# Expert routing by token with rank matmuls, one expert applied to all rows, and logits moved into the second graph layer

## The chip, the cores and the metric

The kernel runs on one core of a Trainium2 chip. The core has a matrix engine (TensorE, "PE" in the profile, with its weight loads shown as "PEld"), a vector engine (VectorE, "DVE"), a scalar engine (ScalarE, "ACT"), GpSimd ("POOL") and a queue engine ("SP") that issues most of the transfers. Each engine works through its own instructions in order and waits on semaphores for the others. The time is device microseconds of that core; three runs of the kernel before took 965.22, 966.63 and 966.90 us, so the median is 966.63 us.

## The reference

A graph of 1250 nodes with 41,250 edges (20,000 random ones in both directions and a loop at every node) carries rows `x` of 512 floats. Two graph layers work on the normalised rows; each takes, at every node, the elementwise maximum over the rows of its neighbours, and two linear maps. Then comes a mixture of eight experts in which each expert chooses its 512 rows ("expert choice").

```python
def graph_conv_max(x, src, dst, W_rel, b, W_root):
    agg = segment_max(x[src], dst, num_segments=1250)
    return agg @ W_rel.T + b + x @ W_root.T
h = relu(graph_conv_max(layernorm(x), ...)); h = relu(graph_conv_max(h, ...))
x = x + h
y = layernorm(x)
probs = softmax(y @ Wr, axis=0)              # [1250, 8], over the rows
vals, idx = top_k(probs.T, 512)              # each expert's rows
hid = gelu(einsum('ecd,edf->ecf', y[idx], W1) + b1)      # 512 -> 256
out_e = einsum('ecf,efd->ecd', hid, W2) + b2             # 256 -> 512
x = x + zeros.at[idx].add(vals[..., None] * out_e)
```

Of equal probabilities the row that comes first is taken, as `top_k` does.

## The kernel before

Rows lie in ten tiles of 125 (`TN`, `NT`). `fast_gnn` does the graph layers, `expert_choice` the experts; a loop behind them runs a general version (`general_gnn`) only if the edges don't fit the fast one, which for these inputs they do.

**The graph layers.** In each layer `first_phase` does the bulk of the maximum with one-hot products on TensorE and gathers on POOL. `second_phase` finishes tile after tile: `own_rest` gathers and merges the last neighbours of a tile, `backs` merges what was put aside, `ended` then turns the tile (`turn`), multiplies it (`conv`) and starts a generator (`finish`) that is taken further, one `yield` at a time, whenever a later tile gets to `ended` (function `on`). In layer two `finish` is `residual` (lines 689 to 704): it loads the tile's rows of `x` and the root part of a tile to come; then adds the positive part of the product to `x` and takes the moments; then scales the row (`normed`) and stores it to `y_d` in HBM; then transposes it into `yT`. All instructions of `fast_gnn` go through the wrapper `InOrder`, which keeps them in the order of the program on their engine and gives them line 34 in the profile. `conv` takes its PSUM bank from `ps_m`, which has two.

Most tiles of layer two's work live in pools that are closed with `gctx`; `acc` (the rows) and `ohs` (one-hot masks; its front half is used again for `yT`) outlive them.

**The experts.** `expert_choice` (lines 1125 to 1370) isn't pinned: the framework's scheduler orders its instructions. It works in two layouts. In the first, partition 16e+r holds expert e, sixteen times the same, and the 1250 rows lie along the free dimension. There it computes, after layer two is done, the logits (12 products of 417 columns, line 1189), the softmax, and the bar, the smallest probability that an expert still takes (lines 1234 to 1254). The bar is searched on the bits of the float: eight rounds, in each of which the sixteen partitions of an expert try sixteen candidates for four bits. A round counts on DVE how many of 1250 values are at least the candidate (line 1242), and a product with `alike` (line 1247) sums over the sixteen.

Then, still along the free dimension, it marks the rows chosen and numbers them by running sums (`tensor_tensor_scan`, lines 1264 and 1267), adds the bias `b2` of all chosen experts to the rows by a product with the weighted mask (line 1275), and stores these rows to `out`. `by_token` transposes probabilities and places into the second layout, with a row per partition. `listed(e)` makes the list of expert e from it: ten one-hot comparisons of the place with a lane number (line 1303) and ten products (line 1304) with a payload of row number and probability, the latter as three bf16 parts.

`gathered` fetches the chosen rows of `y_d` by four indirect transfers of 128 rows (line 1319). `expert` loads the weights (lines 1326 and 1328), transposes the gathered rows (line 1333), multiplies by `W1` (line 1339), takes Gelu on ScalarE (line 1341), multiplies by `W2` (line 1346), scales by the probability on DVE (line 1349) and adds the result into `out` by four indirect transfers (line 1350). Adds of an expert wait until those of the expert before have landed. In the loop of lines 1365 to 1370 the list and the gather of expert e+1 are written ahead of the work of expert e.

Of the kernel before, what the change touches and what calls it, by code (L numbers as in the profile page):

```python
# [9 lines left out]
F32 = mybir.dt.float32  # L10
# [8 lines left out]
P = 128  # L19
# [22 lines left out]
def fast_gnn(tc, ctx, sh, io, y_d):  # L42
# [3 lines left out]

    nc = tc.nc
# [35 lines left out]
    yT = ohs.rearrange("p t n -> p (t n)")[:, :2 * KC * N].bitcast(F32).rearrange("p (c n) -> p c n", c=KC)  # L83
    flag_i = keep.tile([1, 1], I32, name="flag_i")
# [90 lines left out]

    xh = gw.tile([P, NT, 3, D], BF16, name="xh")
# [512 lines left out]
    def residual(t, pm):  # L689
        xt = gk.tile([P, D], F32, name="line", bufs=LINES)  # L690
        sp.dma_start(xt[:TN], x[t * TN:(t + 1) * TN, :])
        fetch_root(1, t + 3)
        yield
        dve.scalar_tensor_tensor(acc[:TN, t, :], pm[:TN], 0.0, xt[:TN], op0=ALU.max, op1=ALU.add)
        moments(t)
        spread(t, t + 1)
        yield
        inverted(t, t + 1)
        yn = gk.tile([P, D], F32, name="line", bufs=LINES)
        normed(t, yn[:TN])  # L700
        stored(y_d[t * TN:(t + 1) * TN, :], yn)
        yield
        turned(yn[:TN], yT[:, :, t * TN:(t + 1) * TN])
        yield

    def second_phase(layer, finish, beside):
# [52 lines left out]
        ready = (8, 9)  # L759
        ended(8, 9)  # L760
        while going:
            on()

# [16 lines left out]
    first_phase(1, 10, late_groups(1) + own_groups(1, range(EARLY)), set(range(NT)), blocks, ready_steps)  # L780
    second_phase(1, residual, lambda: None)
    gctx.close()
    return acc, yT, flag_i
# [341 lines left out]
def expert_choice(tc, ctx, sh, xs, yT, y_d, out):  # L1125


    nc = tc.nc
    ident, node_tile, rows = sh["ident"], sh["TN"], sh["rows"]
    wr, fw1, fb1_t, fw2, fb2 = sh["wr"], sh["fw1"], sh["fb1_t"], sh["fw2"], sh["fb2"]  # L1130
# [4 lines left out]
    TN = node_tile  # L1135
    NT = len(rows)
    CAP = min(512, N)
    R = P // E
    chunks = []
    step = (N + 2) // 3  # L1140
    for c0 in range(0, N, step):
        chunks.append((c0, min(step, N - c0)))
    rp = ctx.enter_context(tc.tile_pool(name="route", bufs=1))
    rp2 = ctx.enter_context(tc.tile_pool(name="route2", bufs=2))
    fwp = ctx.enter_context(tc.tile_pool(name="fwp", bufs=2))
    ps_t = ctx.enter_context(tc.tile_pool(name="fps_t", bufs=2, space=PSUM))
    ps_m = ctx.enter_context(tc.tile_pool(name="fps_m", bufs=3, space=PSUM))
# [3 lines left out]
    wr_s = rp.tile([P, KC, E], F32, name="wr_s")  # L1151
    nc.sync.dma_start(wr_s, wr.rearrange("(c p) e -> p c e", p=P))
    wr_rep = rp.tile([P, KC, E, R], F32, name="wr_rep")
    for c in range(KC):
        nc.gpsimd.tensor_copy(wr_rep[:, c], wr_s[:, c].unsqueeze(2).to_broadcast([P, E, R]))
    alike = rp.tile([P, P], F32, name="alike")
    nc.gpsimd.memset(alike, 1.0)
    alike_v = alike.rearrange("p (e r) -> p e r", r=R)
    nc.gpsimd.affine_select(out=alike_v, in_=alike_v, compare_op=ALU.is_ge, fill=0.0, base=0,
                            pattern=[[-R, E], [0, R]], channel_multiplier=1)  # L1160
    nc.gpsimd.affine_select(out=alike_v, in_=alike_v, compare_op=ALU.is_ge, fill=0.0, base=R - 1,
                            pattern=[[R, E], [0, R]], channel_multiplier=-1)
    lane_i = rp.tile([P, 1], I32, name="lane_ii")
    nc.gpsimd.iota(lane_i, pattern=[[0, 1]], base=0, channel_multiplier=1)
    cand = rp.tile([P, 8], I32, name="rcand")
    for i, shift in enumerate((26, 22, 18, 14, 10, 6, 2, 0)):
        nc.vector.tensor_single_scalar(cand[:, i:i + 1], lane_i, R - 1 if shift else 3,
                                       op=ALU.bitwise_and)
        if shift:
            nc.vector.tensor_single_scalar(cand[:, i:i + 1], cand[:, i:i + 1], shift,  # L1170
                                           op=ALU.logical_shift_left)
    lanes_b = rp.tile([P, P], BF16, name="lanes_b")
    nc.gpsimd.iota(lanes_b, pattern=[[1, P]], base=0, channel_multiplier=0,
                   allow_small_or_imprecise_dtypes=True)

    fb1_s = rp.tile([P, E * FC], F32, name="fb1_s")
    nc.scalar.dma_start(fb1_s, fb1_t)
    fb2_s = rp.tile([P, D], F32, name="fb2_s")
    nc.vector.memset(fb2_s, 0.0)
    for e in range(E):  # L1180
        nc.scalar.dma_start(fb2_s[e * R:e * R + 1, :], fb2[e:e + 1, :])

    prob = rp.tile([P, N], F32, name="prob")
    sm = rp.tile([P, 12], F32, name="sm")
    pls = []
    for k, (c0, w) in enumerate(chunks):
        pl = ps_m.tile([P, D], F32, name="pm")
        for c in range(KC):
            nc.tensor.matmul(pl[:, :w], wr_rep[:, c, :, :].rearrange("p e r -> p (e r)"),
                             yT[:, c, c0:c0 + w], start=(c == 0), stop=(c == KC - 1))  # L1190
        nc.vector.reduce_max(sm[:, k:k + 1], pl[:, :w], axis=AX.X)
        pls.append(pl)
    nc.vector.reduce_max(sm[:, 3:4], sm[:, 0:len(chunks)], axis=AX.X)
    nc.vector.tensor_scalar_mul(sm[:, 4:5], sm[:, 3:4], -1.0)
    nc.vector.memset(sm[:, 5:8], 0.0)
    for k, (c0, w) in enumerate(chunks):
        nc.scalar.activation(prob[:, c0:c0 + w], pls[k][:, :w], AF.Exp, bias=sm[:, 4:5],
                             accum_out=sm[:, 5 + k:6 + k])
    nc.vector.reduce_sum(sm[:, 8:9], sm[:, 5:8], axis=AX.X)
    nc.vector.reciprocal(sm[:, 9:10], sm[:, 8:9])  # L1200
    nc.vector.tensor_scalar_mul(prob, prob, sm[:, 9:10])


    pcol = rp.tile([P, NT, E], F32, name="pcol")
    nc.vector.memset(pcol, 0.0)

    def by_token(of, into, only=None):
        for t in range(NT):
            r = rows[t]
            pt = ps_t.tile([P, KC, P], F32, name="pt")  # L1210
            nc.tensor.transpose(pt[:r, 0, :], of[:, t * TN:t * TN + r], ident)
            nc.scalar.copy(into[:r, t, :],
                           pt[:r, 0, :].rearrange("p (e r) -> p e r", r=R)[:, :, 0])

    by_token(prob, pcol)
    pay = rp.tile([P, NT * E, 5], BF16, name="pay")
    pay4 = pay.rearrange("p (t e) k -> p t e k", e=E)
    lane_f = rp.tile([P, 1], F32, name="lane_f")
    nc.gpsimd.iota(lane_f, pattern=[[0, 1]], base=0, channel_multiplier=1,
                   allow_small_or_imprecise_dtypes=True)  # L1220
    nc.vector.tensor_copy(pay[:, :, 0], lane_f[:, 0:1].to_broadcast([P, NT * E]))
    tile_f = rp.tile([P, NT], F32, name="tile_f")
# [9 lines left out]


    base = rp.tile([P, 1], I32, name="base")
    nc.vector.memset(base, 0)
    jk = rp.tile([P, N], F32, name="jk")
    for i, shift in enumerate((26, 22, 18, 14, 10, 6, 2, 0)):
        last = shift == 0
# [237 lines left out]
```

## Time and profile before

| what | value |
|---|---|
| median of three runs | 966.63 us (965.22 to 966.90) |
| the profiled execution's own time | 959.5 us |
| its span, first to last instruction | 957.8 us |
| TensorE busy, share of the span | 680.2 us, 71% |
| DVE busy | 669.3 us, 70% |
| POOL busy | 531.3 us, 55% |
| ACT busy | 144.1 us, 15% |
| mean granted TensorE clock | 0.914 |

The profiled execution was some 7 us faster than the median of the timed runs; sums that are made on its trace are carried over to the median as differences.

How the profile's lines are read: a line of the timeline gives the start in us from the span's start, the length in us (of the whole group where several instructions are merged), the engine, the line of the kernel, the operation, the tile written and the tiles read, the shape, how many, and in square brackets how long the engine had been idle and what ended that. A line of the groups gives the same names, then busy time in all and mean nanoseconds of one, and the idle time before. In the row of slices each digit is the busy share of a fortieth of the span in tenths. "PEclk" is the clock that TensorE was granted, as a share of its full one. An f32 product appears as two records.

### The profile page before, as it was taken

How to read it: one execution, taken by the hardware profiler on the slowest of the kernel's cores; microseconds unless marked ns; L12 is line 12 of the kernel's file. 1: busy time of each engine (PE TensorE's matmuls, PEld its weight loads, DVE VectorE, ACT ScalarE, POOL GpSimd, SP SyncE). 2: the span in 40 equal slices, each digit the busy share in tenths (PEclk: the TensorE clock that was granted, in tenths of full speed). 3: DMA queues.
4: the chain of work that ended last, by engine and by line, in shares of the span. 5: the costliest groups of instructions: out<-in, count | busy, mean ns of one | idle time of the engine just before them, and what ended most of it. 6: DMA issues, size and time to landing. Idle time of an engine off the chain costs nothing. (4 is left out here: it accounts for less than half of the span.)

```text
span 957.8 us, 8211 instructions
## 1 busy us (share of the span) xinstructions
PE 680.2 (71%) x2367; PEld 359.4 (38%) x2367; DVE 669.3 (70%) x1248; ACT 144.1 (15%) x259; POOL 531.3 (55%) x528
## 2 busy tenths in 40 slices
PE   0000657798889978779888889877666156999992
PEld 0000323454455433335444545433233124454440
DVE  6799759999998866638999989976544773232211
ACT  0700000011000123111110000012222002122210
POOL 5653567776575677145777767777300004464642
PEclk9999978999999989879999999989877575999996
DMA  7428476967686778455978878778623015678773
GB/s 195 134 79 242 143 192 183 195 213 210 209 234 179 232 216 285 139 179 167 204 227 233 281 218 271 211 227 261 206 69 96 0 50 171 160 182 179 174 114 48
DMA packets 71001, 172.64 MB, mean 180 GB/s; under 512 B 12886, under 2 KB 17556, under 8 KB 70946
## 3 DMA queue, kind: packets, MB, share of 16 engines
q0 software_dynamic: 38368, 116.29, 45.5%
q1 hardware_dynamic: 31598, 54.60, 18.2%
q10 hardware_dynamic: 980, 1.12, 0.5%
q8 instruction: 21, 0.34, 0.1%
q14 instruction: 34, 0.28, 0.1%
HBM read 142.48 MB, written 29.45 MB: 180 GB/s over the span
## 5 line engine op out<-in xcount | busy, mean ns | idle before, releaser
L34 PE MATMUL pq<-xh,ohs 126*125 126x512 bf16 x1200 | 296.6, 391 | 66.1 <-DVE acc L34 64.3
L34 POOL DMA_INDIRECT hb<-table_d,late_i x214 | 227.1, 1061 | 128.2 <-issue 50.0
L34 DVE TENSOR_TENSOR acc<-acc,pq 125x1024 f32<-125x1024 f32 x180 | 219.3, 1218 | 45.1 <-PE pq L34 38.6
L34 PEld LDWEIGHTS <-ohs 126*125 126x125 bf16 x1200 | 165.9, 140 | 217.2 <-issue 145.0
L34 POOL DMA_INDIRECT hb<-table_d,nat_i x140 | 148.2, 1058 | 67.7 <-issue 33.2
L1319 POOL DMA_INDIRECT ysel<-y_d,idx x32 | 31.0, 970 | 114.2 <-PE pi L1304 72.8
L34 PE MATMUL pm<-wrel,turn 128*125 128x512 f32 x160 | 82.0, 660 | 14.1 <-DVE acc L34 11.7
L34 PE MATMUL pm<-wroot,turn 128*125 128x512 f32 x160 | 85.9, 619 | 0.0
L34 ACT COPY acc<-pq 125x1024 f32<-125x1024 f32 x20 | 20.2, 1012 | 357.1 <-PE pq L34 357.1
L34 DVE TENSOR_TENSOR wide<-wide,hb 125x1024 f32<-125x1024 f32 (+1 forms) x60 | 71.5, 1191 | 1.8
L1350 POOL DMA_INDIRECT out<-oo,idx x32 | 50.4, 1574 | 25.7 <-DVE oo L1349 13.1
L34 DVE TENSOR_TENSOR hb<-hb 125x1024 f32<-125x1024 f32 (+2 forms) x55 | 52.7, 958 | 16.7 <-DMA hb<-table_d,nat_i 16.7
L1349 DVE TENSOR_SCALAR oo<-pm,val 128x512 f32<-128x512 f32 x32 | 23.9, 750 | 57.4 <-PE pm L1346 57.4
L1339 PE MATMUL pm<-yselT,w 128*128 128x512 f32 x128 | 57.6, 603 | 1.1 <-ACT yselT L1334 1.0
L1346 PE MATMUL pm<-w,hT 128*128 128x512 f32 x128 | 57.7, 599 | 0.0
L34 DVE TENSOR_TENSOR wide<-hb 125x1024 f32<-125x1024 f32 (+1 forms) x40 | 48.1, 1201 | 6.4 <-DMA hb<-table_d,nat_i 6.3
L34 PEld LDWEIGHTS pm<-wrel,turn 128*125 128x125 f32 x160 | 32.0, 210 | 53.3 <-issue 46.5
L34 PE MATMUL pt<-ident,loc 125*20 125x125 f32 x10 | 3.2, 386 | 61.3 <-DVE loc L34 60.9
L1346 PEld LDWEIGHTS pm<-w,hT 128*128 128x128 f32 x128 | 23.7, 190 | 32.8 <-issue 26.5
L34 PEld LDWEIGHTS pm<-wroot,turn 128*125 128x125 f32 x160 | 31.6, 198 | 10.9 <-issue 2.3
L1339 PEld LDWEIGHTS pm<-yselT,w 128*128 128x128 f32 x128 | 24.0, 193 | 29.3 <-issue 27.1
L34 ACT COPY turn<-pt 128x500 f32<-128x500 f32 x40 | 22.9, 574 | 56.6 <-PE pt L34 56.5
(222 smaller groups left out, 696.6 us busy)
## 6 DMA issues: line engine op xcount, KB each, us to landing
w<-in_fw SPq DMA_DIRECT2D x16, 512.0 KB
ohs<-idx_d SPq DMA_DIRECT2D x10, 615.2 KB
ahead<-table_d SPq DMA_DIRECT2D x20, 250.0 KB
root_d<-line SPq DMA_DIRECT2D x20, 250.0 KB
ahead<-root_d SPq DMA_DIRECT2D x20, 250.0 KB
ovf_d<-line SPq DMA_DIRECT2D x18, 224.0 KB
hb<-table_d,late_i POOLq DMA_INDIRECT x214, 5.9
line<-in_x SPq DMA_DIRECT2D x10, 250.0 KB
```

What stands on the lines that cost most here:

```text
L34: made = call(*args, **kwargs)
L1319: nc.gpsimd.indirect_dma_start(out=ysel[:, c, :], out_offset=None, in_=y_d[:, :], in_offset=bass.IndirectOffsetOnAxis(ap=idx[:, c:c + 1], ...
L1339: nc.tensor.matmul(ph[:, :CAP], w1[:, k, f * P:(f + 1) * P], yselT[:, k, :], start=(k == 0), stop=(k == KC - 1))
L1346: nc.tensor.matmul(po, hT[:, f, c * P:(c + 1) * P], w2[:, f, :], start=(f == 0), stop=(f == FC - 1))
L1349: nc.vector.tensor_scalar_mul(oo, po, val[:, c:c + 1])
L1350: add = nc.gpsimd.indirect_dma_start(out=out[:, :], out_offset=bass.IndirectOffsetOnAxis(ap=idx[:, c:c + 1], axis=0), in_=oo[:, :], in_off ...
```

## The change

1. **Logits in layer two.** A new class `Routing` (`head`) holds the routing's constants and results, in the part of `ohs` behind `yT` and in `xh`, which moves to the pool that outlives layer two. `residual` gets a further step that computes the logits of its tile (`head.logits`: four products of 125 columns, a copy on ScalarE, a `reduce_max` on DVE). The rows of `x` are loaded by `fetch_x` three tiles ahead, into six tiles of the spare part of `ohs`. The constants are made in `head.constants`, called before the last two tiles are finished.
2. **One expert on all rows.** Expert 0 (`DENSE = 1`) isn't gathered. `dense_steps` is a generator of 22 steps: 12 with two f32 products each of `yT` by `W1` (500 or 375 columns), with a Gelu after every second, and 10 with a bias product and two f32 products by `W2`, and a copy. Four steps stand at the end of layer two, two behind the exponential, one in each round of the bar search but the first, three among the ranks, and the last six behind the list of expert 1. `own_row` adds the result, times `gate` (the probability if the row is chosen, else zero), to the rows and stores them to `out`, beside expert 1.
3. **The bar.** A round has one DVE instruction less on its way (the shift is taken into the product), and the bar is summed up in two halves, which a product spreads into the second layout. The transposes of the probabilities stand in round one.
4. **Places by token.** The rows chosen are marked and numbered in the second layout: `ranks` sums a mask over the rows ahead of each by products with a triangle and with ones. The scans, the wide masks and the second `by_token` go.
5. **Lists.** `listed` makes the ten one-hot masks of an expert in one DVE instruction of 1280 elements, and its payload in another of 200.
6. **Biases.** `b2` is kept as three bf16 parts in one tile of 96 partitions, and `bias` adds it by one bf16 product into each output of an expert; the ten f32 products of line 1275 go.
7. **Order and buffers.** `expert_choice` is pinned to program order as `fast_gnn` is. Weights have three buffers, and are loaded two experts ahead; the PSUM pool `ps_m` has four banks. `expert` is a generator of two parts (up to Gelu, and the rest).

```diff
@@ fast_gnn
     def residual(t, pm):
-        xt = gk.tile([P, D], F32, name="line", bufs=LINES)
-        sp.dma_start(xt[:TN], x[t * TN:(t + 1) * TN, :])
+        xt = x_tiles[t % 6]
         fetch_root(1, t + 3)
+        fetch_x(t + 3)
         yield
...
         turned(yn[:TN], yT[:, :, t * TN:(t + 1) * TN])
+        yield
+        head.logits(t, ps_q.tile([P, R, D], F32, name="pq")[:, 0, :])
         yield
...
+        if layer == 1:
+            head.constants()
         ended(8, 9)
         while going:
             on()
+            if layer == 1 and len(going) < 2:
+                head.beside(2)
@@ Routing
+    def logits(self, t, pl):
...
+        for c in range(KC):
+            pe.matmul(pl[:, :r], self.wr_rep[:, c].rearrange("p e r -> p (e r)"),
+                      self.yT[:, c, t * TN:t * TN + r], start=(c == 0), stop=(c == KC - 1))
+        act.copy(self.prob[:, t * TN:t * TN + r], pl[:, :r])
+        dve.reduce_max(self.tops[:, t:t + 1], self.prob[:, t * TN:t * TN + r], axis=AX.X)
+    def dense_steps(self):
...
+                    for k in range(KC):
+                        pe.matmul(ph[:, :w], w1[:, k, f * P:(f + 1) * P], self.yT[:, k, c0:c0 + w],
+                                  start=(k == 0), stop=(k == KC - 1))
+                        if k % 2:
+                            yield
+                    act.activation(self.hT[:, f, c0:c0 + w], ph[:, :w], AF.Gelu,
+                                   bias=self.fb1_s[:, e * FC + f:e * FC + f + 1])
@@ expert_choice
+    act.activation(prob, prob, AF.Exp, bias=sm[:, 1:2], accum_out=sm[:, 2:3])
...
+    beside(2)
+    dve.reciprocal(sm[:, 3:4], sm[:, 2:3])
+    dve.tensor_scalar_mul(prob, prob, sm[:, 3:4])
+    act.copy(bp[:B3], fb[:B3])
+    pool.tensor_sub(fb[:B3], fb[:B3], bp[:B3])
+    act.copy(bp[32:64], fb[32:64])
+    act.copy(mid[64:B3], fb[64:B3])
+    pool.tensor_sub(fb[64:B3], fb[64:B3], mid[64:B3])
+    act.copy(bp[64:B3], fb[64:B3])
...
+        pe.matmul(pn, alike, sat, start=True, stop=True)
+        if i == 0:
+            for t in range(NT):
...
+                pe.transpose(pt[:r, 0, :], prob[:, t * TN:t * TN + r], ident)
+                act.copy(pcol[:r, t, :], pt[:r, 0, :].rearrange("p (e r) -> p e r", r=R)[:, :, 0])
+        else:
+            beside()
...
+    def ranks(of):
+        pr = ps_m.tile([P, D], F32, name="pm")
+        flat = of.rearrange("p t e -> p (t e)")
+        pe.matmul(pr[:, :NE], head.low, flat, start=True, stop=False)
+        for t in range(1, NT):
+            pe.matmul(pr[:, t * E:NE].rearrange("p (t e) -> p t e", e=E), head.ones,
+                      of[:, t - 1, :].unsqueeze(1).to_broadcast([P, NT - t, E]),
+                      start=False, stop=(t == NT - 1))
...
     def listed(e):
+        pays = rp2.tile([P, NT, CC, 5], BF16, name="pays")
+        dve.tensor_tensor(pays, pay4[:, :, e, :].unsqueeze(2).to_broadcast([P, NT, CC, 5]),
+                          col4[:, :, e, :].unsqueeze(3).to_broadcast([P, NT, CC, 5]), op=ALU.mult)
+        oh = rp2.tile([P, NT, P], BF16, name="oh")
+        dve.tensor_tensor(oh, head.lanes_b.unsqueeze(1).to_broadcast([P, NT, P]),
+                          lane[:, :, e].unsqueeze(2).to_broadcast([P, NT, P]), op=ALU.is_equal)
...
         for c in range(CC):
             po = ps_m.tile([P, D], F32, name="pm")
+            bias(po, e, P)
...
+    for _ in head.steps:
+        pass
+    for e in range(DENSE, E):
+        work = expert(e, *made, ysel)
         if e + 1 < E:
+            nxt = listed(e + 1)
+            ysel_n = gathered(nxt[0])
+        next(work)
+        if e == DENSE:
+            for t in range(NT):
+                own_row(t)
+        next(work)
```

## The prediction

> **What bounds the kernel now.** I read the page's slices first, for the stages, then the timeline of each engine from 620 us on, because the order of instructions up to there is unchanged by the diff. From the page: the slices of TensorE and its granted clock, and one group.
>
> ```profile
> PE   0000657798889978779888889877666156999992
> PEclk9999978999999989879999999989877575999996
> ...
> L34 POOL TENSOR_TENSOR xh<-acc,xh 125x512 bf16<-125x512 f32 x10 | 11.1, 1149 | 0.0
> ```
>
> One slice is 23.9 us. From slice 30 to 33 (718 to 814 us) TensorE is nearly idle and its clock is down to 0.5 to 0.7: the routing. Then come eight experts with TensorE at nine tenths or more. The timeline of the end of layer two:
>
> ```profile
> 683.70 0.69 DVE L34 SCALAR_TENSOR_TENSOR acc<-pm,line 125x512 f32<-125x512 f32 x1 [3.78 <-DMA line<-in_x]
> 690.51 0.69 DVE L34 SCALAR_TENSOR_TENSOR acc<-pm,line 125x512 f32<-125x512 f32 x1 [4.36 <-DMA line<-in_x]
> ...
> 697.65 1.90 PE L34 MATMUL pt<-ident,acc 125*128 125x125 f32 x8 [5.37 <-DVE acc L34]
> 699.38 5.88 PE L34 MATMUL pm<-wrel,turn 128*125 128x512 f32 x8
> 706.38 3.60 PE L34 MATMUL pm<-wrel,turn 128*125 128x512 f32 x8
> ```
>
> The residual adds of tiles 5 and 6 wait for loads of `x` (8.1 us together); the merges of tile 9 stand behind them on DVE, and `turn(8)`, `turn(9)` behind those. The product of tile 9 (706.38, plus its root part) ends at 710.85; I call this point T0. The routing, by its first and last lines:
>
> ```profile
> 720.60 10.48 PE L1189 MATMUL pm<-ohs,wr_rep 128*128 128x417 f32 x24 [2.35 <-POOL wr_rep L1155]
> 735.32 1.52 DVE L1242 TENSOR_SCALAR_CACHE_REDUCE jk<-prob,bound 128x1250 f32<-128x1250 f32 x1
> 757.72 1.52 DVE L1242 TENSOR_SCALAR_CACHE_REDUCE jk<-prob,bound 128x1250 f32<-128x1250 f32 x1
> 794.10 1.02 POOL L1319 DMA_INDIRECT ysel<-y_d,idx  x1 [72.85 <-PE pi L1304]
> 803.24 1.09 PE L1333 MATMUL pt<-ident,ysel 128*128 128x128 f32 x4 [6.83 <-DMA ysel<-y_d,idx]
> 906.08 1.04 PE L1333 MATMUL pt<-ident,ysel 128*128 128x128 f32 x8
> 908.69 7.13 PE L1339 MATMUL pm<-yselT,w 128*128 128x512 f32 x16 [0.19 <-ACT yselT L1334]
> 915.66 7.22 PE L1346 MATMUL pm<-w,hT 128*128 128x512 f32 x16
> 922.71 1.04 PE L1333 MATMUL pt<-ident,ysel 128*128 128x128 f32 x8
> ```
>
> So: T0 to the bar search 24.5 us; the search 25.1 (to 760.46); from there to the first expert's transposes 42.8; experts 803.24 to 939.51 = 136.3, each 16.63 (906.08 to 922.71) as TensorE alone sets it; then 18.3 to the end of the span.
>
> **Layer two.** Two edits act against each other. `x` is loaded three tiles ahead, which takes both waits away. But each tile now has its logits (8 records of 128x125) on TensorE behind the product four tiles later, a copy on ScalarE, and a `reduce_max` on DVE ahead of the next residual add; and the next-but-one product waits for that add, since `ps_m` has two buffers. So a loop closes: product 4.4 us (639.22 to 643.6), logits, copy 0.27, maximum 0.29, `inverted` 0.35, add 0.7, latencies 0.2. Logits of 125 columns have no row: the f32 records of 417 columns above run at 0.35 us warm, which scales to 0.105; the weight load in front of each is 0.19. Bounds 0.8 and 2.4 us a tile; I take 1.6, eight weight loads, since that is the longer of two overlapping things. Loop 7.8 us.
>
> Placed on the timeline: the add of tile 3 goes from 667.08 to 668.05, of tile 4 from 673.27 to 675.9, of tile 5 stays at 683.7, of tile 6 goes from 690.51 to 691.5. What prefetching gives, the maxima take: merges of tile 9 at 693.4 (692.36 before), `turn(8)` at 698.6. The product of tile 8, as cold as now, ends at 706.9 (706.1); then logits(4), copy, maximum, and only then the add of tile 7 at 709.65, which the product of tile 9 waits for. T0 becomes 714.85: **+4.0**. The DVE constants (nine of 0.15) and the Pool constants lie in the waits of 5 and 35 us there. On SP's queue the `x` loads now stand ahead of the stores of `y`, and the first expert's weights (1 MB) and `fb1` ahead of its last four; they land long before the dense steps at 728. A transfer met uncovered there would cost what the wait for `x` did: 6.2 (issued 684.25, used 690.5).
>
> **T0 to the bar search.** The tail was a ping-pong of `turned` and `normed` of about 2.3 us; with logits it is 2.8, four times (turned 0.6, copy 0.58, logits 1.6), and the last logits end at T0+12.9. Ahead of the exponential, ScalarE's queue now holds a Gelu of the dense expert: it waits for four f32 products of 500 columns (8 x 0.42 = 3.4), T0+16.3; Gelu 0.7; table load 1.28; exponential over 1250 columns 1.4 (417 take 0.61, of which 0.26 is fixed): ends at E = T0+19.8. Reciprocal and scaling 1.2: search at T0+21.0 = 735.9 against 735.32, so **-3.5** for this stage. It saves 10.5 of matmuls and gives most back.
>
> Here a rule weighs. The row: a table load takes 1.28 us, and the work ahead of it at 809.13 ended 0.01 before. The Trainium skill (ScalarE: Activation LUTs, section What ACT_TABLE_LOAD costs) gives 1283 ns plus about 1380 ns of drain for every switch of set. Before, both switches lay in waits; after there are three, two of them (exponential, second Gelu) on the path. By the row 1.28 each as taken; by the page +2.8 in all. I take the row and keep 2.8 in the range.
>
> **The bar search.** An iteration is now 3.16 us (735.32 to 738.48); the shift (0.19) goes, `add` and `ahead` fit in the 0.68 wait for TensorE: 2.97. But in iteration 1 the product `pn` stands behind ten transposes, whose ScalarE copies stand behind: table load 1.28, Gelu 0.7, four bias copies of 0.6 and two Pool subtractions of 1.15 (the group above): 7.0 after E. Ten copies at 0.83 a pair end at E+11.2, where `pn` was wanted at E+5.9. Search ends at E+12.4 + 5 x 2.97 + 1.56 + 1.5 = E+30.3, which is 29.1 long against 25.1: **+3.9**. Call the end B = 764.9. The dense steps between (4 records of 0.31 = 1.25 us) fit even at half clock.
>
> **B to the first expert.** Removed: 14 us of 1250-wide DVE work, ten f32 bias products and their adds. Added: some 19 DVE instructions on 8 to 320 elements (0.2 to 0.5 us by neighbours like the 0.24 of 128x80), two rank groups of eleven small bf16 products (0.1 each), and dense steps between them: 1.95 us each (four f32 records of 0.43 and a bf16 one of 0.22). Chain: masks B+2.9, ranks behind two dense steps B+5.3 and B+8.2, then DVE 3.9 of which the one-hot over 1280 elements is 1.49 (0.16 + 1280/0.96 GHz, the slope of the 1250-wide rows; 0.83 if packed in pairs), list, gather at B+13.7 (now 33.6). The rows would be there at B+22, but six dense steps (11.7) and the next list come first on TensorE: transposes at B+25.9 = 790.8. Against 42.8: **-16.9**. Own rows (7 us of DVE) and their ten stores lie beside the first expert's 17 us; the scatters have about 11 us of slack before a buffer is missed.
>
> **Experts.** Seven instead of eight: 136.3 less 16.6 and less 3.2 (the first, cold one) = 116.4. The bias adds four bf16 products of 0.213 each: 7 x 0.85 = 6.0. Lists were interleaved with transposes and free. Now order is pinned: the list for e+1 stands ahead of the transposes of e on TensorE, and on DVE behind the four `oo` of e-1. TensorE waits for the last `oo` 0.78, `pays` 0.33, one-hot 1.45, 0.1 latency, then ten products 0.7: 3.3 at five boundaries = 16.6. Sum 139.0: **+2.7**. Queued behind the list are transposes and so the whole expert; Pool (12.6 busy) has room.
>
> **Sum.** +4.0 - 3.5 + 3.9 - 16.9 + 2.7 = -9.8 on the span of 957.8. That execution itself took 959.5, below the 965.2 to 966.9 of the runs; I carry the difference over: 966.6 - 9.8 = **956.9**.
>
> **Rivals.** (1) *The logits are cheap*: at 0.9 us a tile, ten times on the chain, -7: 950. For it: weight loads are hidden in wide products; against: at 125 columns they are the longer part. (2) *TensorE's clock*, the slower one. For it: the clock was 0.50 in 735 to 760, and the product at 699.38 ran at half speed after a wait of 5.37. The skill (TensorE: Matmul & The Clock Gate, Part 1) says a window of 3.4 us of idling halves it and one of work restores it. The boundary stall of 2.6 and sparse 3.3 behind it may fill a window: 1.7 x 5 = 8.5; the steps after the bar at half clock: 7.5 (three rank steps +1.9, one warm-up +1.7). All: 973; from 12 of the 16 on, the result is slower. Against: the dense steps fill TensorE to about half in the search, more after. By the row of the experts (1.00 granted, gaps under 1 us) nothing is lost, which I take. (3) *Stores hold the scatters*: if `out` is written over 11 us later than reckoned, each further microsecond counts; 957 to 966. For it the ten stores took 13.3 before; against, the slack.
>
> **Numbers.** Likeliest 0.45 (951 to 963), (1) 0.15, (2) 0.32, (3) 0.08. Measurement tells 0.2% (1.9 us) from no change. Faster: 0.42 + 0.15 + 0.03 + 0.03 = 0.63; slower 0.22 of (2) and 0.04 of the rest = 0.26; same 0.11. Range 945 to 974: it leaves out the low half of (1) and the worst of (2).
>
> **What would show it.** DVE's residual adds free of `in_x` but waiting for ScalarE; T0 near 715; the exponential behind a Gelu; a gap of about 5 us in iteration 1 of the search; first gather some 14 us after the bar; TensorE waiting about 2.6 us for the one-hot at five expert boundaries, period 20.8. Wrong if logits take under 1 us, if the clock falls at the boundaries, or if dense steps delay each `pn`.

## The result

The changed kernel takes 959.99 us (median of 20 runs, 951.97 to 967.42) against 965.15 us (20 runs, 960.15 to 969.75) for the kernel before: a ratio of 0.9937, 95% interval 0.9916 to 0.9958. A second measurement of the same kernel, told below, gave 0.9976 (0.9952 to 1.0), so the gain is real but small. All ratios here leave out executions more than 1.5% above the fastest of their kernel, and where two kernels are compared below in us, the difference is taken between their ratios. The prediction was 956.9 us. The profiled execution took 962.38 us, its span is 960.6 us.

The two profiles differ by 7.2 us before the change begins to act: the first residual add of layer two starts at 641.88 us before and at 649.07 us after, though the diff alters nothing ahead of it but where `xh` lies and a few loads. So stages are compared by their lengths, not by clock times:

| stage | before | after | difference | predicted |
|---|---|---|---|---|
| first residual add to T0 (end of tile 9's product) | 68.96 | 69.04 | +0.1 | +4.0 |
| T0 to the first pass of the bar search | 24.5 | 21.4 | -3.1 | -3.5 |
| bar search | 25.1 | 26.5 | +1.3 | +3.9 |
| bar to the first expert's transposes | 42.8 | 22.7 | -20.1 | -16.9 |
| experts, to the end of TensorE | 136.3 | 154.4 | +18.1 | +2.7 |
| sum | | | -3.7 | -9.8 |

The slices of the page after, 24.0 us each (TensorE, and its granted clock):

```profile
PE   0000657898899978779888889868867888788892
PEclk9999877799999979879999999989978798988897
```

The gap of the routing (slices 30 to 33) is filled: TensorE is at seven and eight tenths there. But the experts behind it, slices 34 to 38, are at 7, 8, 8, 8, 9 where they were at nine tenths throughout, and their clock is at 9, 8, 8, 8, 9. The timeline after, layer two and the routing:

```profile
681.29 0.28 DVE L34 TENSOR_REDUCE ohs<-ohs 128x1 f32<-128x125 f32 x1 [6.40 <-ACT ohs L34]
688.75 0.69 DVE L34 SCALAR_TENSOR_TENSOR acc<-pm,ohs 125x512 f32<-125x512 f32 x1
696.11 0.69 DVE L34 SCALAR_TENSOR_TENSOR acc<-pm,ohs 125x512 f32<-125x512 f32 x1
710.89 1.05 PE L34 MATMUL pq<-ohs 128*128 128x125 f32 x8
...
734.86 0.68 ACT L34 ACTIVATE xh<-pq,ohs 128x500 f32<-128x500 f32 x1 [2.36 <-PE pq L34]
735.56 1.28 ACT L34 ACT_TABLE_LOAD   x1
736.85 1.34 ACT L34 ACTIVATE ohs<-ohs,sm 128x1250 f32<-128x1250 f32 x1
739.49 1.52 DVE L34 TENSOR_SCALAR_CACHE_REDUCE jk<-ohs 128x1250 f32<-128x1250 f32 x1
748.93 0.16 DVE L34 TENSOR_SCALAR step_i<-pn 128x1 int32<-128x1 f32 x1 [2.46 <-PE pn L34]
778.07 2.25 POOL L34 DMA_INDIRECT ysel<-y_d,idx  x1 [26.69 <-issue]
788.68 1.07 PE L34 MATMUL pt<-ident,ysel 128*128 128x128 f32 x8
```

No residual add waits for `x` any more; the maximum ahead of it waits for ScalarE's copy of the logits. The exponential stands directly behind a Gelu and a table load. The first gather goes out 12.1 us after the bar (765.97) instead of 33.6. And the experts:

```profile
800.92 0.75 DVE L34 TENSOR_SCALAR oo<-pm,val 128x512 f32<-128x512 f32 x1 [4.73 <-PE pm L34]
...
819.97 1.65 POOL L34 DMA_INDIRECT out<-oo,idx  x1 [25.61 <-DMA w<-in_fw]
825.02 0.75 DVE L34 TENSOR_SCALAR oo<-pm,val 128x512 f32<-128x512 f32 x1 [14.70 <-DMA out<-oo,idx]
880.16 0.41 PE L34 MATMUL pi<-pays,oh 128*128 128x20 bf16 x10 [2.52 <-DVE oh L34]
884.18 9.47 PE L34 MATMUL pm<-yselT,w 128*128 128x512 f32 x16 [0.68 <-ACT yselT L34]
903.92 0.41 PE L34 MATMUL pi<-pays,oh 128*128 128x20 bf16 x10 [2.52 <-DVE oh L34]
928.17 7.13 PE L34 MATMUL pm<-yselT,w 128*128 128x512 f32 x16 [0.68 <-ACT yselT L34]
```

From list to list (880.16 to 903.92) an expert takes 23.76 us, where 20.8 was reckoned and 16.63 was the period before. TensorE waits 2.52 us for the one-hot, as foreseen; what was not taken into the sum is the next line: the hidden product behind such a wait takes 9.47 us, and 7.13 where no wait stands ahead of it (928.17). The row of SP's queue that the scatters will be seen to depend on:

```profile
790.26 15.92 SPq L34 DMA_DIRECT2D out<-acc  x10
```

The ten stores of the own rows take 15.92 us to issue, so the last leaves near 806 us, and the loads of the weights for the next experts follow it on the same queue.

### The profile page after: what moved, and what is told of

The parts are those of the page before. It is cut to its first block, busy times and chain, and to the rows that moved or that the text cites. A ratio compares the mean times of both kernels' runs of the same rounds, so it can differ in the third digit from the quotient of the medians.

```text
span 960.6 us, 8344 instructions
## 1 busy us (share of the span) xinstructions
PE 709.5 (74%) x2484; PEld 375.0 (39%) x2484; DVE 648.1 (67%) x1164; ACT 154.5 (16%) x274; POOL 535.2 (56%) x543
## 5 line engine op out<-in xcount | busy, mean ns | idle before, releaser
L34 PEld LDWEIGHTS <-ohs 126*125 126x125 bf16 (+1 forms) x1221 | 168.1, 140 | 218.5 <-issue 147.2
L34 DVE TENSOR_SCALAR oo<-pm,val 128x512 f32<-128x512 f32 x28 | 21.0, 750 | 112.4 <-PE pm L34 92.9
L34 POOL DMA_INDIRECT out<-oo,idx x28 | 48.2, 1722 | 77.6 <-DVE oo L34 49.3
L34 PE MATMUL pm<-w,hT 128*128 128x512 f32 x112 | 52.6, 591 | 0.0
L34 POOL DMA_INDIRECT ysel<-y_d,idx x28 | 28.5, 1018 | 40.0 <-issue 33.4
L34 PE MATMUL pt<-ident,acc 125*128 125x125 f32 x80 | 14.0, 318 | 22.3 <-DVE acc L34 21.9
```

What stands on the lines that cost most here:

```text
L34: made = call(*args, **kwargs)
```

## The experiments

Three theories were to be told apart for the 15 us that the experts took beyond the sum: the clock after each boundary's wait, the stores of the own rows that hold the scatters (819.97, 18 us after `oo` was ready), or a limit of Pool and the transfers. Beside it: do the maxima take what the prefetch of `x` gives, and what is the dense expert worth?

The first four kernels ran on one chip. There the kernel before took 964.37 us (25 runs).

**The changed kernel again.**

> The changed kernel again, as the measure for the runs beside it: 960 us, 0.994 of the kernel before; nothing in it is altered.

961.99 us, 0.9976 (0.9952 to 1.0). Its stages: 72.35, 21.4, and experts 157.0. So the same kernel's stages differ by some 3 us between executions; the three that follow are read against this one.

**One maximum.** In `logits` and in `expert_choice`:

```
-        dve.reduce_max(self.tops[:, t:t + 1], self.prob[:, t * TN:t * TN + r], axis=AX.X)
...
-    dve.reduce_max(sm[:, 0:1], head.tops, axis=AX.X)
+    dve.reduce_max(sm[:, 0:1], prob, axis=AX.X)
```

> The ten maxima of 128x125 are taken out of layer two; one maximum over 1250 columns stands ahead of the exponential instead (about 1.5 us in place of 0.2). Theory A, as the prediction had it (the maxima take what the prefetch of x gives): the stage from the first residual add to the end of tile 9's product falls from 69.0 to about 63, and the kernel by 4 to 6 us against the changed one. Theory B, from the trace after (TensorE itself needs 4.5 for the product, 0.9 for the logits and 1.2 for transposes a tile, against a loop of 7.0): only about 0.5 us a tile is to be had, -2.5 in the stage, and with the longer maximum the kernel moves by -1.5 to +1 us.

946.9 us, 0.982 (0.9789 to 0.985): 15 us below the repeat, more than either theory gave. The stage up to T0 is 60.46 us (72.35), the way to the search 17.9 (21.4). Theory B counted only TensorE's own work of 6.6 us a tile against a loop of 7.0, and missed what stands behind an add. The maximum ahead of the add of tile t+1 belongs to logits that stand on TensorE behind the product of tile t+2: in the changed kernel the add of tile 4 starts at 681.75, though its product ended near 669.6. Without the maximum an add is free when its own product is done, and the merges of the last tiles, queued behind the adds on DVE, come early too: the transposes of tiles 8 and 9 start 49.0 us after the first add (693.20) instead of 54.2 in the profile after (703.24) and 57.4 in the repeat. TensorE's waits in 640 to 705 us of this kernel, in all (us, times, longest):

```profile
PE pm L34 <- DMA ahead<-root_d: 3.9, 3, 3.2
PE pm L34 <- DVE acc L34: 3.6, 2, 2.6
PE pt L34 <- DVE acc L34: 2.1, 1, 2.1
```

The waits for DVE are down to 5.7 us (the one at 703.24 alone was 7.50 in the changed kernel), and the next limit shows: the root rows arrive late. In the tail behind T0 the last logits start 8.8 us after it instead of 10.7, because no maximum stands in the ping-pong; the other 1.5 are products that ran warm (7.87 us for the 24 records from the last logits on, 9.34 in the profile after), which the next kernel has too, without this edit.

**`x` late.**

```
         xt = x_tiles[t % 6]
+        fetch_x(t)
         fetch_root(1, t + 3)
-        fetch_x(t + 3)
...
-    for t in range(3):
-        fetch_x(t)
```

> The rows of x are loaded when the residual of their own tile begins, as in the kernel before; all else is as changed. Theory A (the prefetch gives something that the maxima take): DVE waits for x again at tiles 5 and 6 on top of the maxima, the stage from the first residual add to the end of tile 9's product grows by 3 to 6 us, and the kernel by as much. Theory B (the waits were hidden anyway, since the maxima wait for later events): within 1 us of the changed kernel.

963.83 us, 0.9994 (0.998 to 1.0008): 1.7 us above the repeat, with intervals that overlap. The waits come back, but short:

```profile
675.89 0.69 DVE L34 SCALAR_TENSOR_TENSOR acc<-pm,ohs 125x512 f32<-125x512 f32 x1 [1.16 <-DMA ohs<-in_x]
685.57 0.69 DVE L34 SCALAR_TENSOR_TENSOR acc<-pm,ohs 125x512 f32<-125x512 f32 x1 [0.91 <-DMA ohs<-in_x]
```

Three of them, 3.1 us together with one of 1.00 at 654.74, in place of 8.1 before, and the stage is 3.0 us longer (75.39); the tail behind it was 2.8 us shorter in this execution. So in the changed kernel the prefetch is worth about these 3 us at most, which is no more than two executions of one kernel differ by in this stage (69.04 and 72.35). Taken together with the kernel before this one: with `x` early and the maxima away, the stage is 8.5 us shorter than before the change, about the two waits of 8.1; with the maxima in place it is not shorter at all. So the maxima do take what the prefetch gives. The fourth combination, `x` late without the maxima, was not run.

**Own rows early.** `own_row(t)` is moved from behind the first expert's hidden product into the loop that runs the remaining dense steps, after the second list's one-hot:

```
+    def own_rows():
+        done = 0
+        for _ in head.steps:
+            for t in range(done, head.ready):
+                own_row(t)
+            done = head.ready
...
-        if e == DENSE:
-
-            for t in range(NT):
-                own_row(t)
```

> The own rows (ten operations on DVE of 0.68 and their ten stores) follow the dense steps one by one, behind the one-hot of the second list, rather than standing behind the list: the first store leaves about 12 us earlier. Theory A (the stores hold the scatters and that costs): the first scatter starts near 803 us instead of 820, DVE's waits for the scatters of 19.6 us in all are gone, and the kernel gains 3 to 6 us. Theory B (the late scatters lie beside a boundary that TensorE loses to its clock anyway): the scatters move but the boundary between experts 2 and 3 becomes like the others, 23.8 us, and the kernel stays within 1.5 us.

954.69 us, 0.9887 (0.985 to 0.9925): 8.6 us below the repeat by the ratios, theory A and more. The experts take 144.0 us (157.0):

```profile
811.16 1.65 POOL L34 DMA_INDIRECT out<-oo,idx  x1 [15.23 <-DVE val L34]
831.68 0.41 PE L34 MATMUL pi<-pays,oh 128*128 128x20 bf16 x10 [2.52 <-DVE oh L34]
835.13 7.13 PE L34 MATMUL pm<-yselT,w 128*128 128x512 f32 x16 [0.68 <-ACT yselT L34]
852.53 0.41 PE L34 MATMUL pi<-pays,oh 128*128 128x20 bf16 x10 [2.52 <-DVE oh L34]
```

The first scatter starts 8.3 us earlier than in the repeat (819.45), not the 16 expected, but DVE no longer waits for scatters. Measured from first output product to first output product, the second boundary falls from 27.84 to 20.85 us: -7.0. Two more boundaries fall from 23.8 to 20.8, with the same wait of 2.52 us at each: at 831.68 the hidden product behind it runs at 7.13. So the wait of 2.52 us costs the clock at some boundaries and at others not, and 20.8, the period predicted, is what one costs where it doesn't. Of the 13.0 us between these two profiles, then, 7.0 are the boundary with the held scatters (the longer stop and the clock lost behind it) and 5.8 are two boundaries that happened to keep the clock.

That issuing the stores earlier helps is shown. At 819.97 the trace names the load of the next weights (`w<-in_fw`) as what ended the wait, but in the program that load stands behind the scatter. The last store landed at 816.41 by the semaphores of the trace, 3.6 us ahead of the scatter, and here at 807.75, 3.4 us ahead of the one at 811.16. So the stores are the likelier cause; what fills the last 3.5 us stays open.

The next four ran on another chip, on which the kernel before took 1033.71 us (13 runs); most of the difference lies ahead of the first residual add (at 695 to 704 us there), so ratios and stage lengths are read.

**List inside the hidden product.** `expert` yields once more, behind the first half of its hidden product, and the loop becomes:

```
         work = expert(e, *made, ysel)
+        next(work)
         if e + 1 < E:
             nxt = listed(e + 1)
             ysel_n = gathered(nxt[0])
         next(work)
```

> The list and the gathers for expert e+1 stand inside expert e, behind the first half of its hidden product, instead of ahead of its transposes. Theory A (the boundary costs its wait of 2.5 us and a cold clock behind it): no wait for the one-hot, the hidden product at 7.1 us in place of 9.0 to 9.6, the period 23.8 falls to about 17.9 (16.6 as before, 0.9 for the biases, 0.3 for the list), five boundaries give about 29 us: 930 us. Theory B (the period is set by Pool and the transfers, whose work is the same): Pool needs 12.8 us an expert, but the gathers land late, the transposes wait for them, the period is 20 to 22 and the time 940 to 950.

1012.78 us, 0.9779 (0.9673 to 0.9885). The period is 18.2 us at the undisturbed boundaries, theory A; no hidden product there is cold, and Pool carries the same work in 18.2 us, so theory B falls. But one boundary takes 35.2 us:

```profile
884.49 1.65 POOL L34 DMA_INDIRECT out<-oo,idx  x1 [25.41 <-DMA w<-in_fw]
892.07 1.02 POOL L34 DMA_INDIRECT ysel<-y_d,idx  x1 [0.30 <-issue]
896.37 1.94 PE L34 MATMUL pt<-ident,ysel 128*128 128x128 f32 x8 [13.09 <-DMA ysel<-y_d,idx]
```

The first scatters stand at the head of Pool's queue until the own rows are written; the gathers for expert 3 stand behind them, and TensorE waits 13.09 us for those rows.

**Boundary kept busy.** In `listed`, ahead of the list's products:

```
+        if e > DENSE + 1:
+            spare = head.bank()
+            for k in range(10):
+                pe.matmul(spare, pick[:B3, 0, :], bp[:B3, :], start=True, stop=True)
         for t in range(NT):
```

> Ten bf16 products of 96x512 into a spare bank stand ahead of the list at five boundaries, so that TensorE works while it waits for the one-hot; nothing reads them, and the wait itself stays. Theory A (idling costs the clock): the boundary stays at 2.5 us or a little longer, but the transposes take 1.1 and the hidden product 7.1 us, the period is 20.8 to 21.3 as the prediction had it, and five periods give 12 to 15 us: 946 us. Theory B (the hidden product is long for another reason, its operands or the transfers beside it): hidden products stay at 9 us and the time at 960.

1021.12 us, 0.9867 (0.9785 to 0.995). The experts take 149.1 us. At four of the five boundaries:

```profile
917.17 2.32 PE L34 MATMUL pm<-bp,pick 96*128 96x512 bf16 x10
919.85 0.41 PE L34 MATMUL pi<-pays,oh 128*128 128x20 bf16 x10 [0.36 <-DVE oh L34]
923.30 7.13 PE L34 MATMUL pm<-yselT,w 128*128 128x512 f32 x16 [0.68 <-ACT yselT L34]
940.71 0.41 PE L34 MATMUL pi<-pays,oh 128*128 128x20 bf16 x10 [0.36 <-DVE oh L34]
```

The list starts 2.68 us behind the last output product (917.17 to 919.85), as it does in the changed kernel (877.48 to 880.16), but the period is 20.86 us instead of 23.76. Only TensorE's idling differs, so the 2.9 us are its clock: theory A. At the one boundary where the held scatters kept it waiting another 6.15 us, the hidden product was at 9.08 again.

The granted clock confirms it and shows why equal waits cost differently. From 640 us on, every change of the clock in the profiles after, of the own rows early and of this kernel lies a whole number of steps of 3.41 us from the next, and within a step it is either 1.00 or 0.50. Three lines of the profile after, two of the own rows early and one of this kernel, each one step long (start and end, length, busy us of PE, PEld, DVE, ACT and POOL, granted clock, DMA share, GB/s):

```profile
878.69:882.10 3.41, 1.65 (x21) 1.41 (x22) 2.00 (x6) 0.95 (x2) 3.09 (x2) 1.00 0.92 180
882.10:885.51 3.41, 2.73 (x10) 1.79 (x8) 0.00 (x0) 1.30 (x3) 2.69 (x3) 0.50 1.02 246
885.51:888.93 3.42, 3.42 (x5) 1.36 (x5) 0.00 (x0) 0.00 (x0) 0.95 (x1) 0.50 0.71 218
827.58:830.99 3.41, 1.58 (x4) 0.38 (x2) 2.23 (x4) 0.00 (x0) 2.69 (x3) 1.00 0.96 147
830.99:834.40 3.41, 2.43 (x26) 1.95 (x26) 1.22 (x5) 1.47 (x3) 3.08 (x2) 1.00 0.94 216
918.12:921.53 3.41, 2.76 (x26) 1.56 (x24) 2.26 (x6) 0.69 (x2) 2.83 (x2) 1.00 0.90 162
```

In the profile after, the wait ahead of 880.16 falls so that TensorE works for 1.65 us of one step; the next two steps are granted 0.50, and the clock is back only after a step in which it worked throughout. The 6.15 us of work in those two steps would take about half as long at full clock, an estimate of 3.1 us for the loss, beside the 2.9 measured. In the own rows early, the step ends inside the wait ahead of 831.68, both parts hold enough work, and nothing is lost. With the ten products in the wait, no step at the four boundaries has less than 2.4 us of work. How much work a step needs isn't sharp in these figures: 1.58 us kept the clock, 1.65 and 1.77 (ahead of 903.92) lost it.

**No dense expert.** `DENSE = 0`.

> No expert is made dense: all eight go through lists, gathers and scatters, and the own rows are only stored. Theory A (the dense expert fills TensorE where it would wait): an eighth expert at 23.8 us comes on, the dense steps behind the bar and one Gelu and table load leave the path, 5 to 8 us: 973 to 980 us. Theory B (the dense steps cost what they save, since they stand ahead of the first transposes): 956 to 965 us.

1037.38 us, 1.0063 (1.0008 to 1.0119). The changed kernel itself has no run on this chip; its four stages from T0 on add up to 225 us in the profile after and 228.5 in the repeat, and to 232.5 here. So the dense expert is worth some 4 to 8 us by the stages, between the theories (the ratios, which compare across chips, give 8 to 12). An eighth expert adds 23.4 us (177.8 against 154.4); from the search's last pass to the first transposes it is 15.4 us instead of 24.1, because no dense step stands ahead of them, and 3.0 to 5.7 come off ahead of the search (15.65, against 18.65 in the kernel above and 21.4 after). TensorE's clock in the search and behind it is at 0.50 (third column from the right; the windows are the search and the way to the first transposes):

```profile
793.60:817.29 23.69, 7.50 (x24) 5.85 (x24) 17.24 (x57) 3.41 (x13) 4.28 (x9) 0.50 0.48 179
817.29:832.70 15.41, 3.30 (x45) 2.79 (x46) 9.17 (x33) 0.00 (x0) 4.01 (x3) 0.50 0.13 38
```

**List and own rows.** The list inside the hidden product, and own rows in the loop of the dense steps, ahead of the first expert.

> The list inside the hidden product and the own rows beside the dense steps, together. If the stores of the own rows hold the scatters (the first of them 18 us after its data was ready), this shows once the boundaries are gone: 3 to 8 us below the list inside the hidden product alone. If not, the two are within 1.5 us.

995.97 us, 0.9631 (0.9532 to 0.973): 15 us below the list alone. The experts take 127.4 us (144.5), every period is 18.5 or 18.2 us, and the boundary of 35.2 us is gone. The scatter is still held, for 9.20 us, but TensorE does not wait for it:

```profile
869.25 1.65 POOL L34 DMA_INDIRECT out<-oo,idx  x1 [9.20 <-DMA w<-in_fw]
872.67 3.68 PE L34 MATMUL pm<-yselT,w 128*128 128x512 f32 x8
```

The last four ran on a third chip; the kernel before took 1026.32 us there (11 runs). All four profiled executions were longer than the median of their kernel, by 0.4 to 1.9%, so their stages are those of longer executions.

**Three moves** (one maximum, list inside the hidden product, own rows early).

> The three edits that each gave time, together: one maximum over 1250 columns ahead of the exponential, the list inside the hidden product, the own rows beside the dense steps. Theory A (they act in three different stages and add up): experts 127 to 128 us as with the latter two, first residual add to the bar search 78 to 80 us as with the first, and 0.945 of the kernel before (0.9631 for two of them, less 0.0156 for the maximum). Theory B (a transfer takes the place of one: the DMA engines carry the same bytes in 5% less time): the gathers or the weights land late, and the ratio stays at 0.955 or more.

990.86 us, 0.9627 (0.9552 to 0.9702): the expert part of theory A (128.4 us), but not the sum. The ratio is the one that theory B named, but its cause is not there: TensorE waits for gathered rows for 1.1 us in all seven experts, and for no weights. The stage up to T0 is 80.1 us in this profile, and two waits make it so:

```profile
735.70 0.58 ACT L34 COPY ohs<-pt 128x500 f32<-128x500 f32 x1 [16.62 <-remote]
736.34 1.09 PE L34 MATMUL pt<-ident,acc 125*128 125x125 f32 x4 [13.09 <-issue]
745.61 5.92 PE L34 MATMUL pm<-wrel,turn 128*125 128x512 f32 x8 [8.18 <-ACT turn L34]
```

For the first of them the trace names no releaser on TensorE, but ScalarE's copy out of PSUM starts 0.64 us ahead of it, after 16.62 us of idling: TensorE stands behind ScalarE, and for ScalarE's wait the trace names no instruction. Such a stop of TensorE in the tiles of layer two, of 8.2 to 17.3 us, is in all four profiles from this chip, one of 6.5 is in that of the list inside the hidden product on the second, each right behind such a copy of ScalarE, and none is in those of the first chip. What held ScalarE stays open, and with it whether the maximum's 15 us are to be had on every chip.

**Gelu behind.** The calls of `beside` in `second_phase` are left out, and the one behind the exponential runs six steps instead of two.

> As the three moves, and the first four dense steps stand behind the exponential instead of ahead of it, so that ScalarE's queue holds no Gelu between the last logits and the exponential. Theory A (the wait for those products, the Gelu of 0.68 and one table load of 1.28 lie on the path): the search starts 3.4 us earlier (the exponential at the maximum's end, since the table load then lies beside the maximum), and as much comes off the end. Theory B (the dense steps then come later and colder, and stand ahead of the first transposes): the search starts earlier but the transposes do not, and the time is within 1 us of the three moves.

992.31 us, 0.9674 (0.9617 to 0.9731), an interval that overlaps the three moves': theory B by its mechanism. T0 to the search is 15.9 us instead of 17.9, but the search is 25.9 (23.8) and the way to the transposes 26.9 (23.9), with TensorE's clock at 0.86 there instead of 0.97.

**Bias behind.** The four copies and two subtractions are called in the search's third iteration.

> As the three moves, and the four copies and two subtractions that split the biases stand in the third iteration of the bar search instead of ahead of the first. Theory A (the prediction's gap in iteration 1: the transposes' copies stand behind them on ScalarE): the search is shorter by 1.5 to 4 us. Theory B (the first product waits for the transposes themselves and the dense steps, and the subtractions only slow DVE's small operations in another iteration): within 0.5 us.

985.78 us, 0.9599 (0.9542 to 0.9657), an interval that overlaps the three moves'. By stages it changes nothing: search 23.9 (23.8), transposes 23.8 (23.9). Theory B. As with the three moves, the first product `pn` stands behind dense products, which wait for a Gelu (timeline of this kernel):

```profile
810.00 4.48 PE L34 MATMUL pm<-ohs 128*128 128x375 f32 x8 [2.15 <-ACT xh L34]
814.32 0.28 PE L34 MATMUL pn<-sat,ohs 128*128 128x1 f32 x2
```

**All moves.**

> Both of the last two on top of the three moves. If the two gains lie one behind the other, they add (5 us below the three moves); if the transposes of the first expert are set by TensorE's dense steps, which only begin later, less than 2 us.

982.16 us, 0.9594 (0.9546 to 0.9642). The stages from T0 to the transposes are 62.1 us (65.6 with three moves), neither 5 nor under 2 less; the ratio is 3.4 us lower, within its uncertainty. With the biases out of the way the search keeps what its earlier start gives: 22.5 us, at a clock of 0.88 (0.82). This is the fastest version measured by its ratio; the other versions on this chip, and the list and the own rows alone, at 0.9631 on the second, can't be told from it.

## Why the prediction was right, and where not

It said faster, 956.9 us in a range of 945 to 974; measured 960 us. Both the sign and the range hold. The reasoning holds less well than the number: the experts came out 15.4 us longer than the sum had them, and the four stages ahead of them together 9.3 us shorter, of which 3.9 lie in layer two, where the repeat was shorter by only 0.6. That the total missed by no more than 6.1 us of stage lengths is in part luck.

**Experts, +2.7: this step failed; it measured +18.1.** The step took the row of the kernel before, a clock of 1.00 with gaps under 1 us, for boundaries that now wait 2.5 us. The 15.4 us between 139.0 and 154.4 are made up so: four hidden products at 9.0 to 9.6 us instead of 7.13 (+8.9); five times the transposes behind a wait, 3.65 to 4.1 us from their start to the hidden product instead of 3.13 with a warm clock (+3.7); that 3.13 itself, which was 2.61 before, because TensorE now waits 0.68 us for ScalarE's last copy and not 0.19 (0.5 in each of seven experts, +3.7); and biases at 0.70 instead of 0.86 an expert (-1.1). The waits with their lists are 2.95 us at four boundaries and 4.86, with the held scatters, at one: 16.7 in all, and 16.6 were reckoned. So the clock is 12.6 of the 15.4 us: this is rival 2's first half, there estimated at 1.7 a boundary and measured at 2.9 where TensorE was kept busy. The stores, rival 3, were real too: the slack of 11 us was used up and 18 us were needed. In the profile after, the stop at 834.60 (1.9 us longer) was followed by a warm product, because TensorE was idle for just one whole step of the clock (830.90 to 834.31) and worked through most of the next; in the repeat a stop in the same place was followed by a product of 9.19 us, and the early own rows took 7.0 us off that boundary.

The Trainium skill's rule that the prediction cited for rival 2 (TensorE: Matmul & The Clock Gate, Part 1: a window of 3.4 us of idling halves the clock, one of work restores it) bears on the rows in which a wait of 2.52 us with a sparse 3.3 us behind it was followed by 9.47 us once and by 7.13 us at another time. The steps of 3.41 us in the granted clock agree with it in length and in the halving. They differ in one thing, and the measurement decides: a step need not be idle, for one with 1.65 us of work in it was enough to lose the clock.

**Layer two, +4.0: +0.1 and, in the repeat, +3.4.** The closed loop was there: adds 7.0 and 7.36 us apart (681.75, 688.75, 696.11), waiting for ScalarE. The term was mis-sized in the logits, 1.05 us and not 1.6, which is what rival 1 assumed. But rival 1 expected 7 us from it and the stage got 0.6 to 3.9. That the maxima take what the prefetch gives was confirmed on the first chip and is larger than reckoned: without them the stage is 8.6 to 11.9 us shorter.

**T0 to the search, -3.5: -3.1.** The exponential stands behind the Gelu as said. The drain of about 1.38 us that the Trainium skill gives for each switch (ScalarE: Activation LUTs, What ACT_TABLE_LOAD costs) doesn't show: Gelu ends at 735.54, the load starts at 735.56 and the exponential at 736.85. The row of 1.28 was right.

**Bar search, +3.9: +1.3.** The gap was half in iteration 1 (a wait of 2.46 us for `pn`) and half in iteration 0, where it wasn't expected; with 5.14 and 4.69 us they were 4.0 longer than two iterations of 2.93. The others ran at 2.57 to 2.93, not 2.97. Taking the biases away alone didn't shorten the search (with three moves the two iterations take 8.9 us with them and without): the dense products ahead of the first `pn` were in the way as well. With both moved they take 7.4.

**Bar to the transposes, -16.9: -20.1.** The gather at B+12.1 (13.7 reckoned). The transposes came 3.2 us earlier. TensorE's clock was 1.00 from 766 to 789 us: the second half of rival 2, 7.5 us at half clock, did not occur.

**Own rows and stores at nothing.** The cover was the first expert's 17 us. It wasn't enough: the own rows early gave 8.6 us.

## What to carry to other kernels

A wait of TensorE costs itself and what its clock does to the work behind it (2.52 us and up to 2.9 us more here), and the second part depends on where the wait falls in time, so one profile can show either; where a rearrangement turns overlapped small products into a queue order, put them between the halves of a large product rather than ahead of it. A store that must land before the first of a series of scatters belongs ahead of all other traffic, because gathers on the same queue stand behind the scatters. And a small operation on a loop's path (a maximum of 0.28 us) costs what its inputs' engines take to deliver, which one longer operation outside the loop avoids (15 us on the first chip; not to be seen in the ratios of the third).

## What the runs showed of the hardware that was not expected

In the profile after, while Pool subtracts a tile of 96x512 and one of 32x512, operations of DVE on one element a partition with two inputs are slower by several times, and the same operation an iteration later is back at 0.15 us:

```profile
740.86 1.15 POOL L34 TENSOR_TENSOR fb<-fb,bp 96x512 f32<-96x512 f32 x1 [9.69 <-ACT bp L34]
741.12 0.90 DVE L34 TENSOR_TENSOR ahead_b<-base,ohs 128x1 int32<-128x1 int32 x1
743.43 1.14 POOL L34 TENSOR_TENSOR fb<-fb,mid 32x512 f32<-32x512 f32 x1 [1.42 <-ACT mid L34]
743.53 1.06 DVE L34 TENSOR_TENSOR bound<-ahead_b,step_i 128x1 int32<-128x1 int32 x1
746.32 0.15 DVE L34 TENSOR_TENSOR ahead_b<-base,ohs 128x1 int32<-128x1 int32 x1
```

The operation lasts until the subtraction ends (742.01 and 744.57 against 742.02 and 744.59), so the two seem to exclude each other; that was not tried by itself. And the eight records of the logits (four f32 products of 125 columns) with their weight loads take 1.05 us warm: the loads, which the prediction took for the longer part at 0.19 each (1.5 together), overlap the products and each other.
